# Gated cross-attention with a mixture of experts on one core: attention probabilities turned by VectorE and a round trip through DRAM, where TensorE transposed them

## The chip, the cores and the metric

One core of one Trainium2 chip runs the whole program. The time of a kernel is the device time of one execution in microseconds (us). For the kernel before, 18 executions were timed: their median is 912.88 us, from 911.22 to 915.35 us. One more execution was recorded by the profiler.

## The reference, cut to what matters

`x` is (4, 1024, 256) in fp32 and the context is (4, 64, 256). There are 16 heads of 64 columns; then comes a mixture of 8 experts, two for each token.

```python
def attention(q, ctx, w_qs, w_ks, w_vs, w_proj, b_proj):
    qh = einsum('bld,hdk->hblk', q, w_qs)
    kh = einsum('bld,hdk->hblk', ctx, w_ks)
    vh = einsum('bld,hdk->hblk', ctx, w_vs)
    attn = softmax(einsum('hblk,hbmk->hblm', qh, kh))      # over 64 context rows
    out = einsum('hblm,hbmk->hblk', attn, vh) * qh
    return concat_heads(out) @ w_proj.T + b_proj

x = x + tanh(g_xattn) * attention(layernorm(x), ctx, ...)
t = layernorm(x)
logits = t @ gate_w.T                                       # 8 experts
w, sel = softmax of the two largest logits of each token
x = x + tanh(g_ffn) * sum over the two: w * (silu(t @ w1[e]) @ w2[e])
```

## The kernel before, in words

The 4096 tokens are cut into 8 groups of 512, and a group into four strips of 128 tokens. The attention loop goes over the groups (`g`) and in each over four steps (`t`), one for each strip; all engines work in the order that the framework's scheduler made of this loop, and each engine does its instructions strictly in its own order.

In step (g, t), these things are issued:

- `probabilities(g, t)`: 8 score products on TensorE (L401), the row maxima on VectorE (L410), the subtraction of the maxima on VectorE (L412), one exponent over 128x1024 on ScalarE (L415), the sums and their reciprocals on VectorE (L417, L418), and the division on GpSimd (L420).
- `transpose_probabilities` of the strip before: 8 TensorE transposes against the identity (L430) into two PSUM banks, and two ScalarE copies of 128x512 into `aT` (L431).
- `queries` of the next group: products with the query weights into PSUM banks (L386), each copied out by ScalarE into `qT` (L393).
- For the group before, `attend` in steps 1 (both halves of the heads): products with V (L445), and the product with the queries on VectorE (L454); `project` in steps 2 and 3 (L462), added to `x` on VectorE (L469).
- The first layer norm of a later group (`ln_stats`, `ln_norm`: the normalising L295 on VectorE, transposes L299, copies L304), and, for pairs of groups that are through attention, the second layer norm, the router (`logits`, `route`, `place`) and the scatter of token rows into a table in DRAM by GpSimd (`enter`, L582).
- In groups 0 and 1, one part in each step of the clearing of that table: eight transfers of 4620 KB (`clear`, L260), issued by SP.

From group 6 on, pieces of the expert work (`run_slots`) are placed between: weights and token rows come by transfers that SP issues (L802 to L831), the hidden layer is L869 and L877, and the second product is L930. After the attention, nothing but the expert work is left, up to the end.

PSUM is handed out as two double banks (`ps2`: scores) and four single banks (`ps1`: everything else here). Blocks in SBUF are handed out from three shares: "group" (8 blocks), "weight" (7) and "hidden" (2).

All transfers that SP and ScalarE issue draw from eight completion counters, `DMAHW0` to `DMAHW7`, that the framework gives out in turn over both engines, in the scheduler's order. The instruction that issues a transfer first waits until the transfer that held its counter before has landed, whoever issued that one. In the kernel before, ScalarE issues four loads at the start and eight stores of finished groups (L1020); all others are SP's.

Of the kernel before, what the change touches and what calls it, by code (L numbers as in the profile page):

```python
# [8 lines left out]
F32 = mybir.dt.float32  # L9
# [12 lines left out]
def kernel(  # L22
# [64 lines left out]


    blocks = ctx.enter_context(tc.tile_pool(name="blocks", bufs=1))
    shares = {"group": 8, "weight": 7, "hidden": 2}  # L90
    soft = ctx.enter_context(tc.tile_pool(name="soft", bufs=2))
    npool = ctx.enter_context(tc.tile_pool(name="n", bufs=3))
    rows = ctx.enter_context(tc.tile_pool(name="rows", bufs=2))
# [5 lines left out]

    def block(shape, name, share):  # L100
        return blocks.tile(shape, F32, tag=share, bufs=shares[share], name=name)

    def bank(name, spare=False):

# [163 lines left out]
    def ln_stats(groups, name):  # L268
        n = len(groups) * T
        mv = small.tile([P, n, 2], F32, tag="mv", name=f"mv_{name}")  # L270
        for i in range(n):
            st = small.tile([P, 6], F32, tag="st", name=f"st_{name}_{i}")
            first = nc.vector.bn_stats(st, xg[groups[i // T]][:, i % T, :])
            if i == 0 and name[0] == "a":
                tc.keep_in_program_order(first)
            nc.vector.bn_aggr(mv[:, i, :], st)
        rstd = small.tile([P, n, 1], F32, tag="rstd", name=f"rstd_{name}")
        nc.scalar.activation(rstd, mv[:, :, 1:2], AF.Sqrt, bias=eps)
        nc.vector.reciprocal(rstd, rstd)
        return {g: (mv[:, k * T : (k + 1) * T], rstd[:, k * T : (k + 1) * T]) for k, g in enumerate(groups)}  # L280

    def ln_norm(g, stats, name):

        mv, rstd = stats[g]
        nT[g] = npool.tile([P, NC, G], F32, tag="nT", name=f"nT_{name}_{g}")
        first = g == 0 and name == "a"
        keep = None
        if name == "b":
            keep = xg[g]
        elif first:  # L290
            keep = npool.tile([P, T, D], F32, tag="nT", name=f"keep_{name}_{g}")
        pt = [bank(f"pt_{name}_{g}_{c}", first) for c in range(NC)]
        for t in range(T):
            xn = keep[:, t, :] if keep is not None else work.tile([P, D], F32, tag="xn", name=f"xn_{name}_{g}_{t}")
            nc.vector.tensor_scalar(  # L295
                xn, xg[g][:, t, :], mv[:, t, 0:1], rstd[:, t, :], ALU.subtract, ALU.mult
            )
            for c in range(NC):
                nc.tensor.transpose(  # L299
                    pt[c][:, t * P : (t + 1) * P], xn[:, c * P : (c + 1) * P], ident  # L300
                )
        for c in range(NC):
            copy = nc.vector.tensor_copy if first and c else nc.scalar.copy
            copy(nT[g][:, c, :], pt[c])  # L304
# [67 lines left out]
                yield  # L372


    def halves(name, share="group"):

        return [block([P, NP // 2, G], f"{name}_{i}", share) for i in range(2)]

    def of_pair(t, p):
        return t[p // (NP // 2)][:, p % (NP // 2), :]  # L380

    def queries(g, qT, pairs):
        for p in pairs:
            pq = bank(f"pq_{g}_{p}")
            for c in range(NC):
                nc.tensor.matmul(  # L386
                    pq,
                    wq[:, c, p * P : (p + 1) * P],
                    nT[g][:, c, :],
                    start=(c == 0),  # L390
                    stop=(c == NC - 1),
                )
            nc.scalar.copy(of_pair(qT, p), pq)  # L393

    newest = []
# [1 line left out]
    def probabilities(g, t, qT):  # L397

        sc = ps2.tile([P, NP // 2, 2, 2, M], F32, tag="ps2", name=f"sc_{g}_{t}")
        for p in range(NP):  # L400
            nc.tensor.matmul(  # L401
                sc[:, p // 2, :, p % 2, :],
                of_pair(qT, p)[:, t * P : (t + 1) * P],
                kT[g // GB][:, p, :],
                start=True,
                stop=True,
            )
        scv = sc.rearrange("p q r j m -> p (q r j) m")
        mx = small.tile([P, H], F32, tag="mx", name=f"mx_{g}_{t}")
        nc.vector.tensor_reduce(mx, scv, AX.X, ALU.max)  # L410
        pr = soft.tile([P, H, M], F32, tag="pr", name=f"pr_{g}_{t}")
        nc.vector.tensor_tensor(  # L412
            pr, scv, mx.unsqueeze(2).to_broadcast([P, H, M]), ALU.subtract
        )
        nc.scalar.activation(pr, pr, AF.Exp)  # L415
        sm = small.tile([P, H], F32, tag="sm", name=f"sm_{g}_{t}")
        nc.vector.tensor_reduce(sm, pr, AX.X, ALU.add)  # L417
        nc.vector.reciprocal(sm, sm)  # L418
        newest[:] = [
            nc.gpsimd.tensor_tensor(pr, pr, sm.unsqueeze(2).to_broadcast([P, H, M]), ALU.mult).ins  # L420
        ]
        return pr

    def transpose_probabilities(g, t, pr, aT):
        prv = pr.rearrange("p (i j) m -> p i (j m)", j=2)
        n = 512 // P
        for p0 in range(0, NP, n):
            pt = bank(f"pa_{g}_{t}_{p0}")
            for i in range(n):
                nc.tensor.transpose(pt[:, i * P : (i + 1) * P], prv[:, p0 + i, :], ident)  # L430
            nc.scalar.copy(  # L431
                aT[p0 // n][:, :, t * P : (t + 1) * P], pt.rearrange("p (i q) -> p i q", i=n)
            )

    def attend(g, pairs, qT, aT):

        for q in range(pairs[0] // 2, pairs[-1] // 2 + 1):


            po = [bank(f"po_{g}_{2 * q + j}") for j in range(2)]  # L440
            for r in range(2):
                for j in range(2):
                    half = slice(j * M, (j + 1) * M)
                    i = q * 2 + r
                    nc.tensor.matmul(  # L445
                        po[j][r * DK : (r + 1) * DK],
                        vs[half, g // GB, i, :],
                        of_pair(aT, i)[half],
                        start=True,
                        stop=True,  # L450
                    )
            for j in range(2):
                own = of_pair(qT, 2 * q + j)
                nc.vector.tensor_tensor(own, po[j], own, ALU.mult)  # L454

    def project(g, qT, t0):

        pp = bank(f"pp_{g}_{t0}").rearrange("p (t d) -> p t d", d=D)
        for i in range(2):
            t = t0 + i  # L460
            for p in range(NP):
                nc.tensor.matmul(  # L462
                    pp[:, i, :],
                    of_pair(qT, p)[:, t * P : (t + 1) * P],
                    wp[:, p, :],
                    start=(p == 0),
                    stop=(p == NP - 1),
                )
        nc.vector.scalar_tensor_tensor(  # L469
            xg[g][:, t0 : t0 + 2, :], pp, tg[:, 0:1], xg[g][:, t0 : t0 + 2, :], ALU.mult, ALU.add  # L470
        )
# [349 lines left out]
    def load_weights(s):  # L821
# [1 line left out]
        with behind_loads():  # L823
            e = number(s, 0, E - 1)
        w = s - NA
        share = "weight" if s < NA or w % 2 == 0 else "group"
        a = block([P, NC, F], f"w1_{s}", share)
        nc.sync.dma_start(a, w1[bass.ds(e, 1)].rearrange("o (p c) f -> p (o c) f", p=P))
        b = block([P, NF, D], f"w2_{s}", share)
        issued[:] = [  # L830
            nc.sync.dma_start(b, w2[bass.ds(e, 1)].rearrange("o (c p) d -> p (o c) d", p=P)).ins  # L831
        ]
# [16 lines left out]
    def hidden(s, a, xT):  # L849

        n = xT.shape[2]
        if is_wide(s):
            share = "hidden" if (s - NA) % 2 == 0 else "group"
            hT = [block([P, NF // 2, n], f"hT_{s}_{i}", share) for i in range(2)]
        else:
            hT = [block([P, NF, n], f"hT_{s}", "hidden")]
        per_tile = NF // len(hT)
# [143 lines left out]
    def finish(g, step):  # L1001

        qT, aT = held[g]
        if step == 1:
            attend(g, range(NP // 2, NP), qT, aT)
        elif step >= 2:
            project(g, qT, (step - 2) * 2)

    second = {}
    entered = 0  # L1010
# [2 lines left out]
    def after(g, step):  # L1013
# [2 lines left out]
        groups = list(range(g - GB + 1, g + 1))  # L1016
        if step == 0:
            second.update(ln_stats(groups, f"b{g}"))
            for h in groups:
                apart("out", nc.scalar.dma_start(of[h], xg[h]), f"out{h // HG}")  # L1020
        elif step == 1:
            second["logits"] = scores_of([R, E], f"lg_{g}")
            ln_norm(groups[0], second, "b")
# [25 lines left out]


    slots = run_slots(range(NA + OFTEN))
    pieces = {HG + 2: (0, 0, 1, 1), HG + 3: (3, 3, 2, 2), HG + 4: (3, 3, 3, 3)}
    last = None
    assert B * (H // 8) == 2 * T

# [11 lines left out]
    for g in range(NG + 1):  # L1067
        attention_ends = g == NG
        if g < NG:
            qT, aT = qTs[g], halves(f"aT_{g}", "hidden" if g % 2 and g + 1 < NG else "group")  # L1070
            held[g] = (qT, aT)
        for h in parts[g]:
            if h == len(qTs):
                qTs.append(halves(f"qT_{h}"))
        for t in range(T):
            if g < NG:
                pr = probabilities(g, t, qT)
            if last:
                transpose_probabilities(*last)

            b = (g - GB - 1) // GB
            ends, behind = b * GB + GB - 1, (g - GB - 1) % GB * T + t if b >= 0 else -1
            if behind == T:
                placing(ends)
            if g and t == 1:
                attend(g - 1, range(NP // 2), *held[g - 1])
            for h, pairs in parts[g].items():
                queries(h, qTs[h], pairs[t])
            if 0 <= g - 1 < NG:
                finish(g - 1, t)  # L1090
            last = (g, t, pr, aT) if g < NG else None
            if g == 0:
                for _ in range(value_parts[t]):
                    next(pending_values)
# [17 lines left out]
            for _ in range(pieces[g][t] if g in pieces else 0):  # L1112
                next(slots)

    for step in range(2 * T):
        if step == T:
            placing(NG - 1)
# [48 lines left out]
```

## Time and profile before

| what | value |
|---|---|
| median of 18 executions | 912.88 us (911.22 to 915.35) |
| the profiled execution, its own time | 913.85 us |
| span from its first to its last instruction | 912.1 us |
| TensorE matmul (PE) busy | 867.7 us, 95%, 4176 instructions |
| VectorE (DVE) busy | 344.9 us, 38% |
| ScalarE (ACT) busy | 233.9 us, 26%, 334 instructions |
| GpSimd (POOL) busy | 336.7 us, 37% |
| DMA moved | 148.90 MB, mean 163 GB/s |

The span is the core's time between its first and last instruction; 1.75 us of the execution's own time lie outside it. "Busy" counts the instructions of an engine, not the transfers that it issues. One `nc.tensor.matmul` of this kernel is two PE instructions in the profile, and its transposes are one each. A row of a group gives the line, the engine, the operation, the tiles, the shapes, the number of instructions, the busy time and the mean of one, and then the idle time of the engine just before them and who ended it.

### The profile page before, as it was taken

Reading aid. Unit: us, or ns where it says so; the run is one execution under the profiler, and the core shown is the slowest. Engines: PE = TensorE matmul, PEld = TensorE weight load, DVE = VectorE, ACT = ScalarE, POOL = GpSimd, SP = SyncE. Lnnn points to the kernel's source line nnn. Section 1 sums busy time; section 2 is a strip of 40 time slices with the busy share of each in tenths; the row PEclk is TensorE's granted clock in tenths of the full one; section 3 lists DMA queues with packets and bytes.
Section 4 is the critical chain, followed back from the end, with each engine's and each line's share of the span. In section 5 each row is a group of like instructions: output and inputs, shape, how many; then the busy total and the mean of one; then the engine's idle time right before and its main releaser. Section 6 shows DMA issues by size and latency. Waiting matters only on the chain. (4 is left out here: it accounts for less than half of the span.)

```text
span 912.1 us, 12028 instructions
## 1 busy us (share of the span) xinstructions
PE 867.7 (95%) x4176; PEld 663.7 (73%) x4176; DVE 344.9 (38%) x845; ACT 233.9 (26%) x334; POOL 336.7 (37%) x343
## 2 busy tenths in 40 slices
PE   6999999999999997998998899999999999999993
PEld 4555858585858585786877687677777888888882
DVE  4366384669467857552254110111110111111100
ACT  2573252424243325330221112112111111111110
POOL 3042212125512451226237543443434434344342
PEclk9999999999999998999999799999999999999997
DMA  9999995001100334426666776856544475765110
GB/s 201 342 340 341 340 345 188 1 1 67 60 14 1 121 101 126 128 100 206 181 191 197 207 221 196 261 148 201 167 148 135 147 218 175 231 202 180 35 41 24
DMA packets 159987, 148.90 MB, mean 163 GB/s; under 512 B 73768, under 2 KB 149932, under 8 KB 156080
## 3 DMA queue, kind: packets, MB, share of 16 engines
q1 hardware_dynamic: 143728, 117.84, 43.8%
q0 software_dynamic: 9600, 25.25, 8.2%
q10 hardware_dynamic: 6592, 4.98, 1.7%
q8 instruction: 35, 0.57, 0.2%
q14 instruction: 32, 0.26, 0.1%
HBM read 89.67 MB, written 59.41 MB: 163 GB/s over the span
## 5 line engine op out<-in xcount | busy, mean ns | idle before, releaser
L869 PE MATMUL ph<-xT,w 128*128 128x256 f32 (+1 forms) x960 | 244.7, 410 | 4.9 <-issue 4.6
L930 PE MATMUL py<-w,hT 128*128 128x256 f32 x1088 | 243.0, 382 | 0.5 <-issue 0.2
L930 PEld LDWEIGHTS py<-w,hT 128*128 128x128 f32 x1088 | 208.2, 192 | 33.3 <-issue 1.6
L869 PEld LDWEIGHTS ph<-xT,w 128*128 128x128 f32 x960 | 181.6, 191 | 57.3 <-issue 7.8
L877 ACT ACTIVATE hT<-ph 128x1024 f32<-128x1024 f32 (+2 forms) x80 | 71.2, 895 | 396.1 <-PE ph L869 305.7
L420 POOL TENSOR_TENSOR pr<-pr,sm 128x1024 f32<-128x1024 f32 x32 | 61.3, 1917 | 234.1 <-DVE sm L418 174.5
L913 DVE TENSOR_SCALAR x<-py,ids 128x256 f32<-128x256 f32 x68 | 32.8, 483 | 276.2 <-PE py L930 223.9
L386 PE MATMUL pq<-nT_a,wq 128*128 128x512 f32 x256 | 116.0, 597 | 6.7 <-DVE qT L454 4.7
L462 PE MATMUL pp<-wp,qT 128*128 128x256 f32 x512 | 114.3, 380 | 1.9 <-issue 1.9
L462 PEld LDWEIGHTS pp<-wp,qT 128*128 128x128 f32 x512 | 96.9, 190 | 21.7 <-issue 9.1
L915 POOL TENSOR_TENSOR x<-x,x 128x256 f32<-128x256 f32 x68 | 49.1, 722 | 158.1 <-DVE x L913 146.6
L896 POOL DMA_INDIRECT x<-out_dram,ids x68 | 70.0, 1030 | 90.6 <-issue 72.7
L386 PEld LDWEIGHTS pq<-nT_a,wq 128*128 128x128 f32 x256 | 46.2, 190 | 59.4 <-issue 44.5
L582 POOL DMA_INDIRECT table<-x,to_row x64 | 62.6, 979 | 39.8 <-DVE x L571 19.0
L916 POOL DMA_INDIRECT out_dram<-x,ids x68 | 69.2, 1018 | 19.2 <-POOL x L915 17.7
L401 PEld LDWEIGHTS sc<-keys,qT 128*128 128x128 f32 x512 | 62.9, 193 | 12.0 <-issue 11.6
L401 PE MATMUL sc<-keys,qT 128*128 128x128 f32 x512 | 67.5, 279 | 0.0
L431 ACT COPY aT<-pa 128x512 f32<-128x512 f32 x64 | 34.9, 590 | 83.0 <-PE pa L430 72.8
L843 DVE STREAM_TRANSPOSE xT<-x 128x512 f32<-128x512 f32 (+1 forms) x30 | 23.4, 781 | 77.7 <-PE ph L869 38.7
L410 DVE TENSOR_REDUCE mx<-sc 128x16 f32<-128x1024 f32 x32 | 39.0, 1219 | 26.6 <-PE sc L401 26.5
L417 DVE TENSOR_REDUCE sm<-pr 128x16 f32<-128x1024 f32 x32 | 39.0, 1218 | 19.8 <-ACT pr L415 18.7
L454 DVE TENSOR_TENSOR qT<-po,qT 128x512 f32<-128x512 f32 x64 | 40.9, 678 | 12.8 <-PE po L445 11.3
(182 smaller groups left out, 549.4 us busy)
## 6 DMA issues: line engine op xcount, KB each, us to landing
w<-in_L_ffn_w_dram SPq DMA_DIRECT2D x60, 1024.0 KB
table<-empty SPq DMA_DIRECT2D x8, 4620.0 KB
x<-table SPq DMA_DIRECT2D x120, 64.0 KB
out_dram<-x ACTq DMA_DIRECT2D x8, 512.0 KB
x<-in_x_dram SPq DMA_DIRECT2D x7, 512.0 KB
x<-out_dram,ids POOLq DMA_INDIRECT x68
out_dram<-x,ids POOLq DMA_INDIRECT x68
wq<-in_L_xattn_w_qs_dram SPq DMA_DIRECT2D x4, 256.0 KB
```

Of the source, the lines that this page charges most:

```text
L386: nc.tensor.matmul(pq, wq[:, c, p * P : (p + 1) * P], nT[g][:, c, :], start=(c == 0), stop=(c == NC - 1),)
L401: nc.tensor.matmul(sc[:, p // 2, :, p % 2, :], of_pair(qT, p)[:, t * P : (t + 1) * P], kT[g // GB][:, p, :], start=True, stop=True,)
L420: nc.gpsimd.tensor_tensor(pr, pr, sm.unsqueeze(2).to_broadcast([P, H, M]), ALU.mult).ins
L454: nc.vector.tensor_tensor(own, po[j], own, ALU.mult)
L462: nc.tensor.matmul(pp[:, i, :], of_pair(qT, p)[:, t * P : (t + 1) * P], wp[:, p, :], start=(p == 0), stop=(p == NP - 1),)
L582: nc.gpsimd.indirect_dma_start(out=table.rearrange("r (u w) -> (r u) w", w=2), out_offset=bass.IndirectOffsetOnAxis(ap=to_row[:, k, i : i ...
L869: nc.tensor.matmul(ph[:, i, :], a[:, c, f * P : (f + 1) * P], xT[:, c, :], start=(c == 0), stop=(c == NC - 1),)
L877: nc.scalar.activation(hT[f0 // per_tile][:, f1 : f1 + step, :], ph, AF.Silu)
L896: gather = nc.gpsimd.indirect_dma_start(out=acc[t], out_offset=None, in_=outf[:n], in_offset=bass.IndirectOffsetOnAxis(ap=of_rows[:, t, 0, ...
L915: nc.gpsimd.tensor_tensor(acc[t], acc[t], y[:, t], ALU.add)
L916: scatter = nc.gpsimd.indirect_dma_start(out=outf[:n], out_offset=bass.IndirectOffsetOnAxis(ap=of_rows[:, t, 0, 1:2], axis=0), in_=acc[t], ...
L930: nc.tensor.matmul(py[t], hT[f // per_tile][:, f % per_tile, t * P : (t + 1) * P], b[:, f, :], start=(f == 0), stop=(f == NF - 1),)
```

## The change

- `transpose_probabilities` goes, with its TensorE transposes and ScalarE copies. Instead, VectorE turns each strip in blocks of 32x32 (`turn`), into a tile that holds half a group (two strips). ScalarE then stores the half group into a DRAM tensor `turned_rows` (`park`, four transfers of 1024 rows of 256 bytes), in the step after the half's second strip is turned, and reads it back one step later in the order that the product with V needs (`fetch`, four transfers of 256 rows of 1 KB).
- The exponent becomes 16 instructions of 128x64, one for each head, that read the scores from PSUM and take the negated maximum as bias. The subtraction on VectorE goes.
- Both layer norms are normalised on ScalarE (scale and bias), with a small extra VectorE operation for the bias.
- `attend` moves from step 1 to step 2, `project` from steps 2 and 3 to step 3 and to step 0 of the group after next; the store of a finished group moves with it.
- The product with the queries is cut in two, since the columns of `aT` have another order.
- `in_turn` ties the matmuls of scores, queries, `attend` and `project` to the order in which they are written.
- The "group" share has four blocks of double size where it had eight, and `pieces` of the expert work in group 7 are dealt out as 1, 2, 3, 3 where it was 3, 3, 2, 2.

The core of the diff:

```diff
-    shares = {"group": 8, "weight": 7, "hidden": 2}
+    shares = {"group": 4, "weight": 7, "hidden": 2}
...
+        shift = small.tile([P, n, 1], F32, tag="shift", name=f"shift_{name}")
+        nc.vector.scalar_tensor_tensor(shift, mv[:, :, 0:1], -1.0, rstd, ALU.mult, ALU.mult)
...
-            nc.vector.tensor_scalar(
-                xn, xg[g][:, t, :], mv[:, t, 0:1], rstd[:, t, :], ALU.subtract, ALU.mult
-            )
+            with behind_softmax() if name == "b" else nullcontext():
+                nc.scalar.activation(
+                    xn, xg[g][:, t, :], AF.Identity, bias=shift[:, t, :], scale=rstd[:, t, :]
+                )
...
+    def in_turn(matmul):
+        for other in before_it:
+            tc.add_manual_dep(
+                matmul.ins, other.ins.name,
+                mybir.DependencyInfo(mybir.DependencyClass.NoSync, mybir.DependencyReason.DATA),
+                reason="in turn",
+            )
+        before_it[:] = [matmul]
...
-        nc.vector.tensor_reduce(mx, scv, AX.X, ALU.max)
+        nc.vector.tensor_reduce(mx, scv, AX.X, ALU.max, negate=True)
         pr = soft.tile([P, H, M], F32, tag="pr", name=f"pr_{g}_{t}")
-        nc.vector.tensor_tensor(
-            pr, scv, mx.unsqueeze(2).to_broadcast([P, H, M]), ALU.subtract
-        )
-        nc.scalar.activation(pr, pr, AF.Exp)
+        for h in range(H):
+            nc.scalar.activation(pr[:, h], scv[:, h], AF.Exp, bias=mx[:, h : h + 1])
...
-    def transpose_probabilities(g, t, pr, aT):
...
-                nc.tensor.transpose(pt[:, i * P : (i + 1) * P], prv[:, p0 + i, :], ident)
-            nc.scalar.copy(
-                aT[p0 // n][:, :, t * P : (t + 1) * P], pt.rearrange("p (i q) -> p i q", i=n)
-            )
+    turned_rows = dram.tile([NG, 2, P * H * M * 2], F32, tag="turned", name="turned")
+
+    def turn(g, t, pr, turned):
+        nc.vector.transpose(
+            turned[t // 2].rearrange("p b (t j) -> p b t j", t=2)[:, :, t % 2],
+            pr.rearrange("p h m -> p (h m)"),
+        )
+
+    def park(g, a, turned):
+        to = turned_rows[g, a].rearrange("(m b c q) -> c m b q", m=Q, c=P // Q, q=2 * Q)
+        for c in range(P // Q):
+            nc.scalar.dma_start(to[c], turned[a][c * Q : (c + 1) * Q])
+
+    def fetch(g, a, aT):
+        of = turned_rows[g, a].rearrange("(m i r n) -> r m i n", m=Q, r=P // Q, n=S)
+        for r in range(P // Q):
+            nc.scalar.dma_start(aT[r * Q : (r + 1) * Q, :, a * S : (a + 1) * S], of[r])
...
             for j in range(2):
-                own = of_pair(qT, 2 * q + j)
-                nc.vector.tensor_tensor(own, po[j], own, ALU.mult)
+                own = of_pair(qT, 2 * q + j).rearrange("p (a t c q) -> p a c t q", a=2, t=2, q=Q)
+                of = po[j].rearrange("p (a c t q) -> p a c t q", a=2, t=2, q=Q)
+                for a in range(2):
+                    nc.vector.tensor_tensor(own[:, a], of[:, a], own[:, a], ALU.mult)
...
-        if step == 1:
+        if step == 2:
             attend(g, range(NP // 2, NP), qT, aT)
-        elif step >= 2:
-            project(g, qT, (step - 2) * 2)
+        elif step >= 3:
+            project(g, qT, (step - 3) * 2)
...
-    pieces = {HG + 2: (0, 0, 1, 1), HG + 3: (3, 3, 2, 2), HG + 4: (3, 3, 3, 3)}
+    pieces = {HG + 2: (0, 0, 1, 1), HG + 3: (1, 2, 3, 3), HG + 4: (3, 3, 3, 3)}
...
             if last:
-                transpose_probabilities(*last)
+                turn(*last, turned)
+            if t == 0 and g:
+                park(g - 1, 1, turned)
+                if g > 1:
+                    finish(g - 2, T)
+                    leave(g - 2)
+            elif t == 1 and g:
+                fetch(g - 1, 1, held[g - 1][1])
+            elif t == 2 and g < NG:
+                park(g, 0, turned)
...
-            if g and t == 1:
+            if g and t == 2:
                 attend(g - 1, range(NP // 2), *held[g - 1])
...
+            if t == 3 and g < NG:
+                aT = block([P, NP, G], f"aT_{g}", "group")
+                held[g] = (qT, aT)
+                fetch(g, 0, aT)
```

## The prediction

> **What bounds the kernel now.** I read the page's busy times and its 40 slices first.
>
> ```profile
> PE 867.7 (95%) x4176; PEld 663.7 (73%) x4176; DVE 344.9 (38%) x845; ACT 233.9 (26%) x334; POOL 336.7 (37%) x343
> ...
> PE   6999999999999997998998899999999999999993
> ...
> ACT  2573252424243325330221112112111111111110
> ...
> DMA  9999995001100334426666776856544475765110
> ```
>
> TensorE is the bound from end to end: only 912.1 - 867.7 = 44.4 us of the span are not matmul. ScalarE has room. The DMA row shows what decides below: in the first six slices (to some 150 us) the DMA engines are full. The DMA part says with what, and the timeline of SP shows the one stretch:
>
> ```profile
> 27.17 103.11 SPq L260 DMA_DIRECT2D table<-empty  x8
> ```
>
> ```profile
> core 0: us, PE busy (x) PEld busy (x) DVE busy (x) ACT busy (x) POOL busy (x), PEclk, DMA share, GB/s
> ...
> 120.00:140.00 20.00, 19.04 (x113) 12.54 (x112) 15.43 (x31) 9.22 (x13) 3.63 (x2) 1.00 1.09 340
> 140.00:160.00 20.00, 20.00 (x111) 16.28 (x110) 10.43 (x19) 6.77 (x11) 4.07 (x3) 1.00 0.51 161
> 160.00:180.00 20.00, 19.45 (x124) 11.18 (x123) 13.55 (x25) 8.58 (x14) 3.80 (x2) 1.00 0.00 0
> ```
>
> Eight clears of 4620 KB at 340 GB/s take 13.9 us each, and the last ends where the traffic falls, near 140 + 161/340 x 20 = 149.5 us. Counting the trace's packets of these transfers (4480 each), the third to the eighth clear end at 76.9, 90.8, 104.7, 120.0, 133.9 and 150.7 us. Nobody waits for them before; now see when ScalarE did the exponents of group 1 (its timeline):
>
> ```profile
> 73.65 1.06 ACT L415 ACTIVATE pr<-pr 128x1024 f32<-128x1024 f32 x1 [0.85 <-DVE pr L412]
> ...
> 81.69 1.06 ACT L415 ACTIVATE pr<-pr 128x1024 f32<-128x1024 f32 x1 [1.07 <-DVE pr L412]
> ...
> 91.19 1.06 ACT L415 ACTIVATE pr<-pr 128x1024 f32<-128x1024 f32 x1 [1.07 <-DVE pr L412]
> ...
> 103.42 1.06 ACT L415 ACTIVATE pr<-pr 128x1024 f32<-128x1024 f32 x1 [1.08 <-DVE pr L412]
> ```
>
> The groups give the prices:
>
> ```profile
> L430 PE MATMUL pa<-ident,pr 128*128 128x128 f32 x256 | 35.0, 278 | 5.9 <-POOL pr L420 5.9
> ...
> L843 DVE STREAM_TRANSPOSE xT<-x 128x512 f32<-128x512 f32 x22 | 15.6, 710 | 73.7 <-PE ph L869 35.0 <-remote 18.8 <-issue 12.3
> ...
> L278 ACT ACTIVATE rstd_b<-mv_b,eps 128x8 f32<-128x8 f32 x4 | 1.2, 300 | 0.0
> ...
> L525 ACT ACTIVATE lg<-lg 128x64 f32<-128x64 f32 x4 | 1.0, 256 | 8.1 <-DVE lg L524 8.1
> ```
>
> **What goes.** The 256 transposes, 35.0 us of PE, and the 5.9 us in which PE waited for GpSimd before them: -40.9 us, all on the path. ScalarE loses 64 copies (34.9 us) and 32 large exponents (33.8 us), VectorE 32 subtractions (39.1 us) and 64 norms (24.5 us). None of these ends the path, and I take nothing for them.
>
> **What comes on VectorE.** 32 turns of 128x1024: L843 takes 0.71 us at 512 and 0.975 us at 768 elements, so about 1.24 us, 39.7 us in all. The product with the queries becomes 128 instructions of 256 columns, by the rows of 256 columns (0.41 to 0.48 us) 52 to 62 us where it was 40.9. VectorE stays near its 38%. Cost 0, hidden under TensorE; if the cover is gone, the slower release of the `po` banks costs some 2 us a group.
>
> **What comes on ScalarE.** An exponent of 128x64 with a bias by partition: L278, which has one, takes 0.300 us at 8 elements; L877 rises by 0.83 ns an element (596 to 1023 ns from 512 to 1024), so 0.347 us. Neighbours overlap: seven copies of L346 stood in 1.98 us at a mean of 0.378, so 0.095 less each. A strip takes 16 x 0.25 = 4.0 us (by L525 without bias 2.6; with no overlap 5.6) where it took 1.06. With queries' copies (8 x 0.58), norms (up to 8 x 0.5), their copies (2.4), 16 transfers to issue (x 0.47, as L147) and table loads, ScalarE has some 36 us in a group of 44 to 49 us. It fits, but in series: its waits are what count.
>
> **What moves.** `attend`, `project` and the store of a group (0.38 us to issue, L1020) come one step later. After the last strip that is one step of some 12 us in which TensorE must have expert pieces; there are nine early slots of 14 us each, so I cost it at 0, and without them at 12 us.
>
> **The waits for the clears, the largest term.** The built program of the changed kernel says which counter each transfer waits for (order alone, no time). The second transfer of the first fetch of group 0 gets the counter of the fourth clear; the second park of group 0 those of the fifth and sixth; the second fetch of group 0 that of the seventh; the first park of group 1 that of the eighth. These stand on ScalarE ahead of the exponents of the strips (1,0), (1,1), (1,2) and (1,3). Queued behind each wait are also the copies that free TensorE's PSUM banks, so TensorE stops within four banks. With clears as before, (1,0) starts after 90.8, (1,1) after 120.0, (1,2) after 133.9 and (1,3) after 150.7 us, against 73.65, 81.69, 91.19 and 103.42.
> The parks and fetches themselves lengthen the clears: 4096 packets of 256 bytes and 1024 of 1 KB in each half group, which took 21.6 and 50.2 ns each before, are 5.5 + 3.2 us of all 16 engines, 17.4 us for group 0. I take 10 of it, so the eighth clear ends at 161. Four issues (1.9), three norms and a copy (2.1) later strip (1,3) starts at 165: 61.5 us late. By then the kernel before had also done one more projection half (7.1 us of L462), and seven strips of transposes (7 x 1.09 = 7.6) are already in the 40.9. The term is 61.5 + 7.1 + 7.6 = +76 us. Ends: 65 with no lengthening, 90 with all of it and slower packets.
> Here the row for 256-byte packets is one of reads, and stores of 256 bytes are not in the trace. The Trainium skill, DMA: Bandwidth & Descriptors, Specifications, speaks against this step: it asks for at least 512 bytes for line rate and says that smaller transfers become read-modify-write. No run here shows it. If it doubled the stores' time (an estimate from that sentence), group 0 would add 11 us to the clears and the forecast would be 1002 us.
>
> **The wait for the fetch in each later group.** After the scores of strip 1 TensorE has two queries' pairs (3.6 us) and the scores of strip 2 (1.9), then `attend`. ScalarE after the same scores: maxima on VectorE 1.2, exponents 4.0, four fetches to issue 1.9, and data some 3.5 us later (1 KB packets, 64 an engine): 10.6 us. TensorE stands 5 us, in groups 2 to 5: +20 us. Ends: 0, with exponents at 2.6 us and an order that fills the gap; 45 with 5.6 us and slow parks.
>
> **The clock.** A stop of this size has a price of its own in the trace (timeline of PE, then the stages):
>
> ```profile
> 357.74 1.97 PE L430 MATMUL pa<-ident,pr 128*128 128x128 f32 x8 [5.13 <-POOL pr L420]
> ```
>
> ```profile
> 340.00:360.00 20.00, 14.87 (x98) 13.55 (x100) 13.43 (x25) 10.54 (x13) 3.79 (x2) 0.90 0.53 152
> 360.00:380.00 20.00, 19.84 (x123) 13.51 (x116) 14.01 (x22) 8.25 (x11) 4.28 (x3) 0.93 0.41 117
> ```
>
> After 5.13 us of idling the granted clock fell: 0.10 x 20 + 0.07 x 20 = 3.4 us lost. I take half of that for each of four stops, +7 us (0 to 14). The Trainium skill, TensorE: Matmul & The Clock Gate, What's actually happening, puts the fall to half rate at an idle window of about 3.4 us. By that rule every 5 us stop would pay in full, 14 us, and the forecast would be 998.
>
> **Groups 6 and 7.** There the counters are shared with SP's loads of weights and tokens. SP holds a load until TensorE frees its block (L828's longest wait before was 18.7 us), and ScalarE's parks and fetches of groups 6 and 7 wait behind such loads. TensorE's fill there is thin, the queries being done. +15 us (0 to 40). The coarser "group" share I cost at nothing, since weights are loaded three slots ahead; without that cover it is one second product, 7 us.
>
> **Sum,** against the profiled execution's 913.85 us, which is 1 us over the median: 913.85 - 40.9 + 76 + 20 + 7 + 15 = 991 us.
>
> **Rivals.**
> A, the clears alone: the later stops are filled, 913.85 - 40.9 + 76 = 949 us. For it: PE's list has transposes of both norms to move forward. Against: `in_turn` fixes most of the order. Chance 0.25.
> B, ScalarE becomes the bound: exponents nearer 0.35 us apart, +1.6 us on 32 strips in series with the waits, and the upper ends of the stops: 1040 us. Chance 0.18.
> C, the other side: ScalarE never meets the clears. It needs the clears landed, or other counters, by the time the first fetch stands ready, about 70 us; for that they would have to be twice as fast as the 340 GB/s of the trace, or the counters dealt otherwise. Then what is left is -40.9 with stops of 0 to 42 us: 873 to 915 us. The DMA row and the built order both speak against it. Chance 0.05.
> The forecast itself has 0.52.
>
> **How the numbers follow.** 991 us is the likeliest case. The range from 944 to 1040 takes in A and reaches B's centre; it leaves out C and the slower half of B. A measurement of this kernel tells about 0.2%, 1.8 us, from no change. All cases but C are slower: 0.95; of C's 0.05, 0.01 is within that bound.
>
> **What would show it.** Right: ScalarE idle before L458 and L453 until clears land between 75 and 165 us, TensorE's slices 3 to 7 far below 9, idle of PE before `po` ended by transfers in each group, and no L430. Wrong: exponents of strip (1,3) before 150 us; or PE idle under 60 us in the first 180. If the strips of 16 exponents take over 5 us, B is on. If PE's busy time does not fall by 35 us apart from clock, the first term is wrong.

## The result, and the profile after

The changed kernel takes 1038.84 us (median of 8 executions, 1035.14 to 1040.36) where the kernel before takes 912.68 (50 executions): a ratio of 1.138, 95% interval 1.136 to 1.139. The forecast was 991 us, 944 to 1040. The direction was right and the range just holds the time, but the loss is 126 us where the sum said 77 (991 less the 913.85 of the profiled execution).

The page of the changed kernel, busy times and slices (span 1042.9 us; the profiled execution took 1044.9 us, some 6 us over the median):

```profile
PE 878.3 (84%) x3920; PEld 645.8 (62%) x3920; DVE 332.4 (32%) x854; ACT 302.8 (29%) x812; POOL 335.9 (32%) x343
...
PE   7955019898988889667967999999999999999994
...
ACT  3751033546462553145400321111111111111100
...
PEclk9978559998998989796988999999999999999998
DMA  9999994444255434683776465878655546666210
```

Two things are to be seen. TensorE has 256 instructions fewer, the transposes, and yet it is busy longer: 878.3 us, where 867.7 less 35.0 would be 832.7. And its idle time rose from 44.4 to 1042.9 - 878.3 = 164.6 us. The hole in slices 3 to 6 is the one that was forecast. What was not forecast is that the slices from the 7th to the 22nd, most of them at 9 before, are now at 6 to 9, and the clock row with them.

The timeline of ScalarE shows the first hole (start, length, then the idle time before and who ended it):

```profile
99.27 3.38 ACT L433 ACTIVATE pr<-sc,mx 128x64 f32<-128x64 f32 x16 [16.17 <-issue]
...
111.45 20.63 ACTq L453 DMA_DIRECT2D turned<-turned  x4
...
168.43 1.33 ACT L433 ACTIVATE pr<-sc,mx 128x64 f32<-128x64 f32 x6 [1.61 <-DVE mx L430]
```

The strips (1,0) and (1,3) are exponentiated from 99.27 and 168.43 us; the forecast was "after 90.8" and 165. Four parks, 20.63 us from the first issue to the end of the last, stand between: they are among those that wait for clears. The waits of TensorE, totals over the run, then times and the longest:

```profile
PE po L470 <- DMA aT<-turned: 73.5, 10, 45.7
PE pt_b L307 <- ACT x L303: 17.5, 4, 11.4
PE sc L421 <- ACT pr L433: 13.4, 2, 11.4
```

The 45.7 us are the hole. The other nine waits of `po` are 27.8 us in all; the waits of `pt_b`, the second norm, were in no step of the prediction.

### The profile page after: what moved, and what is told of

It reads as the page before. It is cut to its first block, busy times and chain, and to the rows that moved or that the text cites. A ratio compares the mean times of both kernels' runs of the same rounds, so it can differ in the third digit from the quotient of the medians.

```text
span 1042.9 us, 12257 instructions
## 1 busy us (share of the span) xinstructions
PE 878.3 (84%) x3920; PEld 645.8 (62%) x3920; DVE 332.4 (32%) x854; ACT 302.8 (29%) x812; POOL 335.9 (32%) x343
## 5 line engine op out<-in xcount | busy, mean ns | idle before, releaser
L961 PE MATMUL py<-w,hT 128*128 128x256 f32 x1088 | 240.5, 379 | 0.2 <-issue 0.2
L433 ACT ACTIVATE pr<-sc,mx 128x64 f32<-128x64 f32 x512 | 110.1, 363 | 81.0 <-DVE mx L430 64.7
L470 PE MATMUL po<-aT,vs 64*64 64x512 f32 x256 | 63.2, 839 | 79.5 <-DMA aT<-turned 73.5
L406 PE MATMUL pq<-nT_a,wq 128*128 128x512 f32 x256 | 120.8, 615 | 1.7 <-DMA x<-in_x_dram 1.7
L470 PEld LDWEIGHTS po<-aT,vs 64*64 64x64 f32 x256 | 14.6, 173 | 115.8 <-issue 102.4
L406 PEld LDWEIGHTS pq<-nT_a,wq 128*128 128x128 f32 x256 | 48.3, 199 | 59.2 <-issue 54.7
L413 ACT COPY qT<-pq 128x512 f32<-128x512 f32 x64 | 37.1, 608 | 146.6 <-issue 53.1
```

Of the source, the lines that this page charges most:

```text
L406: in_turn(nc.tensor.matmul(pq, wq[:, c, p * P : (p + 1) * P], nT[g][:, c, :], start=(c == 0), stop=(c == NC - 1),))
L433: nc.scalar.activation(pr[:, h], scv[:, h], AF.Exp, bias=mx[:, h : h + 1])
L470: in_turn(nc.tensor.matmul(po[j][r * DK : (r + 1) * DK], vs[half, g // GB, i, :], aT[half, i], start=True, stop=True,))
L961: nc.tensor.matmul(py[t], hT[f // per_tile][:, f % per_tile, t * P : (t + 1) * P], b[:, f, :], start=(f == 0), stop=(f == NF - 1),)
```

## The experiments

A comparison is always with the kernel before, on the same chip. Four kernels ran on a chip where that one took 919.4 us (scalar_only, clear_pool, spread, pf_pool), the others where it took 912.3 to 912.4; so ratios are compared, and a ratio of 0.001 is 0.9 us.

### The change cut by stages

Three kernels put TensorE's transposes back, for the groups in `TENSOR`, and keep all else of the change: the ScalarE part, the moved steps, `in_turn`.

```diff
+    TENSOR = range(first, NG)      # first = 0, 2, 6
...
-                turn(*last, turned)
+                (transpose_probabilities if last[0] in TENSOR else turn)(*last, turned)
...
-                park(g - 1, 1, turned)
+                if g - 1 not in TENSOR:
+                    park(g - 1, 1, turned)
```

The fetches and the first park go the same way, and `aT` is then the tile that the transposes' copies fill, from step 1 on.

> The changed kernel with no strip turned through memory: all groups go back to 8 transposes a strip on TensorE and copies by ScalarE, into the same columns of aT; no parks and fetches are left. Everything else of the change stays: ScalarE's exponents and norms, attend and project a step later, the matmuls tied in order. The first of three kernels that cut the change by stages. Theory (the road through memory is the loss): 915 to 930 us, since the ScalarE part alone was at a ratio of 1.005 and the moved steps were costed at nothing. Rival (the moved steps and the tied order make the stops): over 945 us.

Measured: 960.62 us, ratio 1.053 (1.051 to 1.056). The rival holds. With no byte going through memory, 48 us of the loss are there.

> As the kernel with no turned strip, but groups 0 and 1 go through memory as in the change; groups 2 to 7 are transposed on TensorE. Its difference to that kernel is the early term by itself, with its share of the 40.9 us of transposes (10) taken off. The prediction's sum says 76 - 10 = 66 us more, theory: 60 to 72 us more, so some 985 us. Rival (the early stop is given back later, as other work moves into it): under 40 us more.

Measured: 1019.67 us, ratio 1.118 (1.115 to 1.121): 59 us more, just under what was expected. The early stop is real and is not given back.

> As the changed kernel, but groups 6 and 7 are transposed on TensorE; groups 0 to 5 go through memory. Its difference to the kernel with only groups 0 and 1 through memory is the price of groups 2 to 5, and the changed kernel's difference to it is that of groups 6 and 7. The prediction's sum says 27 - 20 = 7 us for groups 2 to 5 and 15 - 10 = 5 us for groups 6 and 7. Theory now (the clock falls to half for 7 to 10 us after each stop of 3 us or more, and stops have followers): some 25 to 35 us for groups 2 to 5, so 1010 to 1020 us, and some 20 to 35 us for groups 6 and 7. Rival (the whole miss is the shared counters of groups 6 and 7): 990 to 1000 us here.

Measured: 1027.83 us, ratio 1.128 (1.125 to 1.131). Groups 2 to 5 cost 8 us, as the prediction's sum had it and not as expected here; groups 6 and 7 cost the rest, 1.138 - 1.128, some 10 us (9 by the ratios, 11 by the medians).

One more kernel does the opposite, the kernel before with the ScalarE part alone:

```diff
-        nc.vector.tensor_tensor(pr, scv, mx.unsqueeze(2).to_broadcast([P, H, M]), ALU.subtract)
-        nc.scalar.activation(pr, pr, AF.Exp)
+        for h in range(H):
+            nc.scalar.activation(pr[:, h], scv[:, h], AF.Exp, bias=mx[:, h : h + 1])
...
-            nc.vector.tensor_scalar(xn, xg[g][:, t, :], mv[:, t, 0:1], rstd[:, t, :], ALU.subtract, ALU.mult)
+                nc.scalar.activation(xn, xg[g][:, t, :], AF.Identity, bias=shift[:, t, :], scale=rstd[:, t, :])
```

> The kernel before with only the ScalarE part of the change: exponents by heads with the maximum as bias, and both norms on ScalarE. The turn by TensorE, attend in step 1 and everything else are as before. Theory (ScalarE has room, what counts is its waits): within 5 us of the kernel before, 908 to 918 us. Rival (a strip's exponents of 3.4 us in series and norms behind exponents make TensorE wait): 925 to 950 us, with idle of TensorE before the transposes of the norms and of the probabilities.

Measured: 925.63 us, ratio 1.005 (1.003 to 1.008), some 5 us. So the account, on a kernel before of 912.4 us, is:

| what | measured | the prediction's sum |
|---|---|---|
| ScalarE part alone | +5 | 0 |
| everything else but the road through memory | +43 | 0 (12 without cover) |
| the road in groups 0 and 1 | +59 | 76 - 10.2 = +66 |
| the road in groups 2 to 5 | +8 | 20 + 7 - 20.5 = +6.5 |
| the road in groups 6 and 7 | +10 | 15 - 10.2 = +5 |
| sum | +126 | +77 |

(Rounded; 10.2 and 20.5 are the shares of two and four groups in the 40.9 us that the transposes gave back.) The road through memory costs some 78 us, the sum had 77. The miss lies in the second row. The first two rows together lengthen the profiled span by 47 us (912.1 before, 959.1 with nothing turned): 5 by the scores of (2,0), 24 from there to those of (6,0), and 18 after them. The timelines of TensorE show what it is: the step 1 of a group, from the scores of strip 1 to those of strip 2 and what follows. First the kernel before (group 4), then the kernel without any turned strip (group 4), then the changed kernel (group 3):

```profile
213.09 1.95 PE L401 MATMUL sc<-keys,qT 128*128 128x128 f32 x16
...
215.85 1.95 PE L445 MATMUL po<-aT,vs 64*64 64x512 f32 x16
219.18 3.70 PE L386 MATMUL pq<-nT_a,wq 128*128 128x512 f32 x8 [1.38 <-DVE qT L454]
222.81 1.95 PE L445 MATMUL po<-aT,vs 64*64 64x512 f32 x16
224.69 2.05 PE L401 MATMUL sc<-keys,qT 128*128 128x128 f32 x16
226.57 1.04 PE L430 MATMUL pa<-ident,pr 128*128 128x128 f32 x8
```

```profile
236.06 1.95 PE L421 MATMUL sc<-keys,qT 128*128 128x128 f32 x16
...
238.71 3.60 PE L406 MATMUL pq<-nT_a,wq 128*128 128x512 f32 x8
242.15 1.95 PE L421 MATMUL sc<-keys,qT 128*128 128x128 f32 x16
250.27 1.97 PE L458 MATMUL pa<-ident,pr 128*128 128x128 f32 x8 [6.18 <-POOL pr L438]
```

```profile
242.03 1.95 PE L421 MATMUL sc<-keys,qT 128*128 128x128 f32 x16
243.81 3.60 PE L406 MATMUL pq<-nT_a,wq 128*128 128x512 f32 x8
247.25 1.95 PE L421 MATMUL sc<-keys,qT 128*128 128x128 f32 x16
252.03 2.06 PE L307 MATMUL pt_b<-ident,x 128*128 128x128 f32 x8 [2.83 <-ACT x L303]
```

Before, `attend` stood in step 1 between the scores and filled it: 224.69 - 213.09 = 11.6 us, and the next work was ready. With `attend` gone to step 2, step 1 keeps two pairs of queries. It is 6.1 us long with transposes and 5.2 us without, while step 0, which got a `project`, is 16 us. A strip's maxima, exponents, sums and division take 1.2, 3.4, 1.5 and 1.9 us, 8 us in all, and they also wait for their turn on each engine. In the middle kernel, for the strip of that step:

```profile
238.42 1.23 DVE L430 TENSOR_REDUCE mx<-sc 128x16 f32<-128x1024 f32 x1 [1.25 <-PE sc L421]
...
240.93 1.28 ACT L433 ACT_TABLE_LOAD   x1
242.22 3.38 ACT L433 ACTIVATE pr<-sc,mx 128x64 f32<-128x64 f32 x16
...
248.32 1.90 POOL L438 TENSOR_TENSOR pr<-pr,sm 128x1024 f32<-128x1024 f32 x1 [9.47 <-DVE sm L436]
```

From the end of the scores (238.0 us) to the end of the division (250.2) that is 12.2 us. Before, the same way took 9.9 us (215.0 to 224.9), and the 11.6 us of step 1 covered it. So TensorE comes to step 2 before the softmax, and whatever of the strips stands first there is waited for: the divided strip in the middle kernel, the second norm here, in other groups the fetched data. The waits for the divided strip add up to 28.5 us without the road, and to 5.7 us in the kernel with the ScalarE part alone (totals, times, longest):

```profile
PE pa L458 <- POOL pr L438: 28.5, 9, 6.2
```

```profile
PE pa L431 <- POOL pr L421: 5.7, 5, 1.9
```

In the first of these two TensorE's idle time is 959.1 - 882.2 = 76.9 us, in the second, on another chip, 928.1 - 878.5 = 49.6; of the 27.3 us between them this wait is 22.8. From the scores of one group to those of the next (group 4) it is 45.2 us before, 53.8 with nothing turned, and 54.5 in the changed kernel. That the thin step is the cause of these waits is read from the timelines. No run refilled it, by two pairs of queries more in step 1 for example, and none dropped the tied order, which forbids other tied products to move into the gap. Nor has a run the moved steps without the ScalarE part, whose longer exponents (3.38 us where one of 1.06 stood) are in the 12.2 us: that part is worth 5 us where step 1 is full, and may be worth more where it is thin. How the 43 us divide over the moved steps, the tied order, the coarser shares, the other dealing of the expert pieces and this interplay stays open, and so does how much of the 18 us behind (6,0) belongs to the end of the attention.

### The early term: counters or traffic?

The clears on GpSimd's queue, whose completion counters are its own:

```diff
-            nc.sync.dma_start(
+            nc.gpsimd.dma_start(
                 table.rearrange("(i p r) w -> i p r w", p=P, r=r)[i],
```

> The changed kernel with one edit: the eight clears of the table are issued on GpSimd's queue instead of SP's. They move the same bytes at the same steps, but no longer hold any of the eight counters that ScalarE's transfers draw from. Theory (ScalarE stands because of the shared counters): the exponents of strip (1,3) start by about 115 us where they started at 168.4 us, the 45.7 us wait before the first product with V falls under 12 us, and the time falls from 1038.8 to 970 to 990 us. Rival (the full DMA engines: parks and fetches are slow among the clears whatever counters they have): strip (1,3) still after 150 us and a time over 1020 us. Second rival (GpSimd is held by issuing the clears, and the divisions come late): strips of group 0 and 1 late by GpSimd, time between.

Measured: 1065.69 us, ratio 1.159 (1.154 to 1.164). It is slower and answers another question. On SP the clears stood behind the loads of the inputs. On GpSimd they were issued from 4.9 us on and ran beside those loads: ScalarE's line for the next norm's deviation, with 50.83 us of idle time before it, is at 69.14 us, and the scores of (0,0) start at 81.2 us where they start at 33.9. The shared counters were not tested.

```diff
-            if g < 2:
-                clear(g * T + t, 2 * T)
+            if g < 4 and t % 2 == 0:
+                clear(g * 2 + t // 2, 2 * T)      # and each waits for the division of its strip
```

> The changed kernel with the eight clears still on SP, but one in every second step of groups 0 to 3 (each issued after the division of its strip), where it was one in every step of groups 0 and 1, all queued by 27 us. Each clear then has some 25 us to land before the next, and its counter comes up again some nine transfers later. Theory (counters held by queued clears): nearly all of the early term goes, strip (1,3) at 110 to 120 us, time 965 to 985 us. If the bandwidth of the clears is the cause, this kernel too is faster, but the one with the clears on GpSimd's queue is not; if neither matters, it stays at 1039.

Measured: 1014.51 us, ratio 1.104 (1.098 to 1.110), some 31 us better than the change.

Then both edits together, with GpSimd's own order in place of SP's wait for the division:

> The changed kernel with the clears on GpSimd's queue, one in every second step of groups 0 to 3 behind the division of that step's strip: no shared counters with ScalarE, and not ahead of the input loads, which the first try on GpSimd's queue delayed. Theory (the clears cost TensorE some 76 us by their counters): strip (1,3) at 105 to 115 us, no wait of more than 8 us before the first product with V, the scores of (2,0) at 112 to 122 us where they start at 176.2, and 960 to 985 us by this chip's own before of about 919 (a ratio of 1.045 to 1.07 where it was 1.138). Rival (the early term is traffic beside the parks and fetches, or the step structure itself): the scores of (2,0) stay after 130 us, as in the kernel with the clears spread on SP (131.2), and the ratio stays over 1.09.

Measured: 1005.56 us, ratio 1.102 (1.097 to 1.106): no different from the clears spread on SP, although no counter is shared now. The scores of (2,0) start at 131.3 us, not 176.2, but TensorE still waits 18.9 and 10.9 us before the first `po` of two groups. Two stages show why; the first of these stops lies in them (length, then PE, PEld, DVE, ACT and POOL busy, then clock, DMA share and GB/s):

```profile
90.00:100.00 10.00, 0.00 (x0) 0.00 (x0) 2.93 (x4) 5.90 (x29) 1.89 (x1) 0.53 0.97 323
100.00:110.00 10.00, 2.29 (x6) 0.61 (x10) 1.22 (x1) 1.27 (x7) 0.00 (x0) 0.50 1.07 325
```

The DMA engines are full with a clear while the parks and fetches are due, and one issue of a park took 6.63 us there. So the early term has two parts. Where all clears are queued at once, transfers wait for their counters: in the changed kernel's trace the last packets of the fourth, fifth, sixth and eighth clear end at 94.2, 109.6, 124.2 and 157.8 us, and the transfers that get their counters next are issued at 96.0, 111.5, 126.0 and 158.4. Spreading gives back 31 us, but it thins the traffic along with these waits and does not part the two. The rest, towards 59, is at least in part plain traffic. It also moved: groups 2 and 3 took 57.3 and 59.6 us here, with clears beside them, where they take 50.3 and 56.7 in the changed kernel.

```diff
-            nc.scalar.dma_start(to[c], turned[a][c * Q : (c + 1) * Q])
+            nc.gpsimd.dma_start(to[c], turned[a][c * Q : (c + 1) * Q])      # and the fetches
```

> The changed kernel with parks and fetches issued by GpSimd instead of ScalarE; the clears stay on SP. Their completion counters are then others than those of SP's loads, and ScalarE waits for no transfer of them. Theory: the waits for the clears (about 76 us) and for the loads of groups 6 and 7 (16.4, 10.3 and 21.5 us on ScalarE) go, the stops for the fetched data stay, some 960 us. Rival: GpSimd, which divides each strip, stands behind the parks and fetches and hands the divisions on late, so the loss only moves to GpSimd: over 1000 us, with TensorE or VectorE waiting for the division.

Measured: 1039.92 us, ratio 1.130 (1.125 to 1.134). Early it gains (the scores of (2,0) start at 130.4 us), then it loses: TensorE waits 20.2 us before the first `po` of group 2 and 10.9 to 14.1 us in each later group. The rival's size was right and its reason was not: GpSimd waits for VectorE's sums before the division (185.9 us in all), and what TensorE waits for is the fetched data.

This kernel says more on the early term than it was made for. All clears are queued on SP as in the change, and their packets even run until 187.7 us; yet the scores of (2,0) start at 130.4 us, as with spread clears (131.2 and 131.3), where the changed kernel has 176.2 and the kernel with nothing turned 114.9. So some 46 of these 61 us go when parks and fetches no longer wait for the clears' counters, with the clears themselves issued as before. What part the other queue has in it, which moves the same bytes in packets of 4096 bytes, was not tested.

### The stops of the later groups

```diff
-        for h in range(H):
-            nc.scalar.activation(pr[:, h], scv[:, h], AF.Exp, bias=mx[:, h : h + 1])
+        nc.vector.tensor_tensor(pr, scv, mx.unsqueeze(2).to_broadcast([P, H, M]), ALU.subtract)
+        nc.scalar.activation(pr, pr, AF.Exp)      # and both norms on VectorE
```

> The changed kernel with the ScalarE part undone: the subtraction on VectorE, one exponent of 128x1024 and both norms on VectorE as before; turning, parks, fetches, moved steps and the clears on SP stay. Theory (in groups 2 to 7 TensorE stands for norms and fetches that are queued behind exponents on ScalarE): the waits of pt_b for ScalarE (17.5 us) go, the waits of po in groups 2 to 5 shrink by 2 us each, and with them the half clock: 20 to 35 us less than the changed kernel, ratio 1.10 to 1.115. Rival (the stops are set by the road through memory alone): within 8 us of the changed kernel. The early term (clears) stays in both.

Measured: 1042.25 us, ratio 1.141 (1.137 to 1.146), the rival. The 17.5 us of `pt_b` for ScalarE go, and in the same places TensorE now waits for VectorE: 17.6 us for `lT`, 9.9 for the norm, 6.3 for `qT`. Taking one releaser away brings out the next.

```diff
         for t in range(T):
+            if t == 1 and g:
+                fetch(g - 1, 1, held[g - 1][1])
             if g < NG:
                 pr = probabilities(g, t, qT)
...
-            elif t == 1 and g:
-                fetch(g - 1, 1, held[g - 1][1])
```

> The changed kernel with the second fetch of a group issued ahead of the exponents of the strip of its step instead of behind them. Theory (in groups 2 to 5 the fetched data is late because its issue stands behind a strip's exponents, not because of the transfer): the waits of 4.05, 4.12 and 8.35 us of po for aT in groups 2, 4 and 6 fall under 1 us, the clock there stays at 1.00, and with it some 10 to 25 us go: 1015 to 1028 us. Rival (the transfer itself is slow): the waits stay over 3 us. Second rival (the exponents now come late by the four issues): the strips' scores wait, and the time is as it was or longer.

Measured: 1048.7 us, ratio 1.150 (1.147 to 1.153). The waits of `po` for the data in groups 2 and 4 fell from 4.05 and 4.12 to under 1 and 1.70 us, so the issue stood behind the exponents, as said. Group 2 became 3.9 us shorter, but group 4 stayed at 54.8 us, with a wait of 4.09 us for VectorE, and from the scores of (6,0) to those of (7,3) it took 110.2 us where the changed kernel took 99.8. Again the stop stays and changes its name.

```diff
+                for _ in range(5):
+                    in_turn(nc.tensor.matmul(spare, wq[:, 0, :P], wq[:, 0, :512], start=True, stop=True))
                 attend(g - 1, range(NP // 2), *held[g - 1])
```

> The changed kernel with five products that nobody reads (128x512, 0.88 us each at full clock, 4.4 us in all) tied into TensorE's order just before the first product with V of each group, where TensorE stands 4 to 8 us in groups 2, 4 and 6. They add work and remove none. Theory (a stop of 3 us and more brings half clock for 7 to 10 us, about 4 us lost each time): the granted clock between 180 and 400 us rises from 0.91 to over 0.96 and the time falls by 8 to 25 us, 1014 to 1031 us. Rival (the clock is not set by the stops, or the stops cost only their own length): 1035 to 1060 us, the products' own time added wherever TensorE did not stand.

Measured: 1055.61 us, ratio 1.156 (1.153 to 1.160). The clock between 180 and 400 us rose from 0.91 to 0.96, as the theory had it, but the time rose as the rival had it. Where the stop is before `po` the products were free or a little better (group 2 took 48.7 us and not 50.3, group 4 54.5 as before); where it is before the second norm they came after it and cost 2.6 and 4.5 us (groups 3 and 5). In these two profiles 10 us more are lost behind the scores of (7,3), where TensorE's longest wait for fetched data is 12.4 us and was 3.9.

```diff
-            nc.scalar.dma_start(to[c], turned[a][c * Q : (c + 1) * Q])
+            (nc.gpsimd if g >= 5 else nc.scalar).dma_start(to[c], turned[a][c * Q : (c + 1) * Q])      # and the fetches
```

> The changed kernel with the parks and fetches of groups 5 to 7 alone on GpSimd's queue, with completion counters other than those of SP's loads. Theory (in groups 6 and 7 ScalarE stands 16.4, 10.3 and 21.5 us for loads that share its counters, which cost TensorE about 45 us with the clock): ScalarE's issues no longer stand, and 20 to 40 us go, 1000 to 1020 us. Rival (TensorE has nothing else to do there, or the longer road over GpSimd, with 10.9 to 14.1 us of waiting a group where all parks and fetches were on GpSimd, eats it): 1030 to 1045 us.

Measured: 1035.78 us, ratio 1.135 (1.133 to 1.137), whose interval overlaps that of the change. In the changed kernel ScalarE does stand there, as this line from its timeline shows (two issues in 21.48 us):

```profile
518.13 21.48 ACTq L453 DMA_DIRECT2D turned<-turned  x2
```

But without these waits TensorE stands 13.8 us for the fetched data and 11.4 us for the product with the queries in the same stretch.

No kernel tried is faster than the kernel before.

## Why the prediction was right or wrong

- **What goes, and VectorE: right.** PE has 256 instructions fewer. The turn takes 1.245 us (1.24 forecast), the halved product 0.41 us, VectorE is at 32%. TensorE's waits for the product with the queries before `po` are 5.5 us (0.8 before), so its cost is small but not nothing.
- **ScalarE: right in kind.** A strip of exponents takes 3.38 us (4.0 forecast, 2.6 to 5.6), so rival B is off. The part is worth 5 us on its own, and undoing it in the changed kernel wins nothing. Its issues were too cheap: four parks take 4.5 us, not 1.9.
- **The waits for the clears: the size was right, the mechanism only in part.** 168.4 us for strip (1,3) against 165, and 59 us against 66 net. Rivals A (949 us) and C are out: A left out the later losses, and C needed ScalarE to miss the clears. But the prediction put the whole term on the counters. With no shared counter, and the clears spread, the kernel wins 33 us and not 59; the stages with full DMA engines say that the road competes with the clears there as well.
- **The wait for the fetch: right in length, wrong in its cause.** The prediction counted the two pairs of queries and the scores ahead of `attend` and found TensorE 5 us early; the trace has 4.05 and 4.12 us for the data in groups 2 and 4, and 2.83 us for the norm in groups 3 and 5. Yet the kernel with no fetch stands at this point of groups 1 to 6 too, 4.8 to 6.2 us in four of them and 1.6 in two. The early arrival belongs to the moved steps. That the road's net price in groups 2 to 5 came out right (8 against 6.5 us) is partly luck: it is a difference between two kernels that both stop there.
- **The moved steps: the step that failed.** They were costed at 0, or 12 us without cover, because only the end of the attention was looked at, where one step more needs other work. What counts is each group: `attend` left step 1 and nothing came in. All else but the road and the ScalarE part measured 43 us, and by the timelines the thin step is where most of the added idle time lies. That the measured time is still inside the range is luck here: the range reached up to 1040 us for a slower ScalarE (rival B), which did not come.
- **The clock: mis-sized.** 7 us were given (1.7 for each of four stops). In the changed kernel the 2.83 us stop of group 3 was followed by half clock until 261.6 us. Three single microseconds of it, the stop, the first work after it, and the end:

```profile
251.00:252.00 1.00, 0.00 (x0) 0.00 (x1) 1.00 (x2) 1.00 (x3) 0.00 (x0) 0.67 1.12 217
252.00:253.00 1.00, 0.97 (x5) 0.68 (x6) 0.53 (x2) 1.00 (x3) 0.30 (x1) 0.50 1.15 213
...
261.00:262.00 1.00, 1.00 (x3) 0.53 (x2) 1.00 (x4) 0.00 (x0) 0.47 (x1) 0.71 0.89 195
```

  That is some 10 us at 0.50, so 5 us lost; after the 4.05 us stop of group 2 it was 7 us (203.6 to 210.4), so 3.4 lost. The rule that the prediction weighed (the Trainium skill, TensorE: Matmul & The Clock Gate, What's actually happening) was nearer than the half price taken from one row: the stops of groups 2 to 5 each brought 6.8 to 10.2 us at half clock, some 15 us lost in all, where 7 were given and 14 stood for that rule. Its window of about 3.4 us is no bound in this trace, where the clock fell some 2.1 us into the stop of group 3. Over the run PE is busy 45.6 us more than its work explains. Up to 11 of these are there in the kernel with the ScalarE part alone too, at a clock of 0.981, on a slower chip. By the trace's clock records PE is busy for 73.3 us at half clock, before for 13.6; half of the difference, 30 us, is what the clock adds to its busy time. Much of it lies in the early term and in groups that the sum costed by their length, so it is not to be added to the account above.
- **Groups 6 and 7: low, inside its ends.** 10 us net against 5. The waits on shared counters are as described, 16.4 and 21.5 us on ScalarE, but taking them away wins some 2 us, and 5 by the ends of the two intervals: other waits stand behind them.
- **Stores of 256 bytes: the doubled cost is not seen.** The rule of at least 512 bytes (the Trainium skill, DMA: Bandwidth & Descriptors, Specifications) would have made it 1002 us, by the prediction's estimate. The parks' 256-byte packets took a median of 18 ns and a mean of 19.6, those of 256-byte reads 18 and 21.6. The nearest row was the right one. For the fetches it was low: the packets of 1 KB on ScalarE's queue took a mean of 67.7 ns, where the row had 50.2.

## What to carry to other kernels

When a piece of work is moved to another step, add up what the bounding engine has left in every step of the loop, and compare it with the latency of the chain that the next step waits for; here 5.2 us of products stood against a softmax of 8 us and more. If the first wait in a place is taken away and the time stays, look for what the step lacks and not for the next releaser: four edits here only changed the name of the waiter. And when a transfer shares a chip with a long one, ask twice: who holds its completion counter, and who has the DMA engines.

## What the runs showed of the hardware that was not expected

- A stop of TensorE of 2.8 to 4 us is followed by 7 to 10 us at half of its clock, though it works most of that time. In the changed kernel's clock records each stretch at half clock, but the one at the end, is a whole number of 3.41 us (6.83, 10.24, 13.65 and so on), so that a stop is paid for in steps of 1.7 us. Filling the stops with products that nobody reads raised the clock and not the speed of the kernel.
- Issuing a transfer of 1024 rows of 256 bytes took ScalarE 1.1 us each where four stood in a row (4.5 us), and 6.63 us for one with the DMA engines full; loads of 1 KB rows took 0.62 us each.
- The queue of the same transfer decides what it runs beside: the clears, moved from SP's queue to GpSimd's, overtook the input loads, and the first scores started 47 us later.
